# Tap loads over 119 partitions, layer-1 rows kept on chip, and the sums of the gates spread out, in a two-layer graph kernel on one core

## The chip, the cores and the metric

The kernel runs on one core of a Trainium2 chip, as one program. The metric is the device time of one execution in microseconds (us). The kernel before took 2211.03 us (median of 3 runs, 2210.8 to 2211.14).

## The reference, cut to what matters

There are 128 graphs (B) of 128 nodes (N) with 256 channels (D), all in float32. Layer 0 works on every node, layer 1 on the first 25 nodes of each graph.

```python
h = relu(layernorm(x))
# layer 0
c = relu(bn1(conv1x1(h)));  c = bn2(conv17(c))             # 17 taps along the nodes
x_conv = relu(c + h)
s = h @ w_se.T + b_se                                      # 3 numbers per node
A = exp(-|s_n - s_m|^2) * adj
x_nmp = A @ relu(h @ w_msg.T + b_msg)                      # "neighbours"
gi = concat(x_conv, x_nmp) @ w_ih.T + b_ih;  gh = h @ w_hh.T + b_hh
r, z = sigmoid(gi_r + gh_r), sigmoid(gi_z + gh_z)
x = x + (1 - z) * tanh(gi_n + r * gh_n) + z * h
# layer 1: for 5 groups g of nodes (25, 9, 7, 6 and 6 of the first 25 nodes)
h = relu(layernorm(x));  a = D^-1/2 (adj_g + I) D^-1/2
x[:, group] += w[g] * relu(a @ (relu(a @ (h @ W1[g]) + b1) @ W2[g]) + b2)
```

## The kernel before

**Units.** Layer 0 goes over 32 quads of 4 graphs (`q`). A quad's x is a tile of 128 partitions (4 graphs x 32 nodes) and 4 slices of 32 nodes; slice 0 holds the nodes that layer 1 needs. Layer 1 goes over 8 blocks of 16 graphs, that is 4 quads each (`blk`).

**Stage A** (L371-422, `stage_a`), once per quad, in two batches of 16: load x (`load_xa`, four DMAs on SyncE's queue), layernorm on VectorE (`moments`, `normalize`), transposes (`ph`, L390), the 1x1 convolution (`pc`, L401), and a real Fourier transform of length 80 along the nodes (`pf`, L412). h is written to DRAM (`hTd`).

**Tap weights** (L439-475, `tap_weights`), beside stage A of the first batch: the 17 taps of the convolution are brought to the 80 Fourier rows with matmuls whose contraction runs over the taps (`pw`, L455). Four of them work at the same time[...]. `load_taps` (L430) brings 64 input channels at a time into `wt`: in each of four bands of 32 partitions, 17 partitions (one per tap) take 16 channels. The 17th tap is a DMA of its own (L436). The products are copied to `ws` on VectorE and ScalarE and written to DRAM (`wfd`, L467, 4 KB runs).

**Stage B** (L478-533) multiplies in the Fourier domain, once per batch. **`early`** (L622) computes the neighbours (`pse`, `pm`, `pd`, `px`, L565-620) of each quad beside A and B and writes them to DRAM (`xmd`).

**Stage C** (L637-829), per quad: `stage_n` loads h and the neighbours back (`hT`, `xm`); `stage_c` does the inverse transform (`pi`), the transposes back (`pc`, L677), the gate products (`p`, L698), the product of h for the new state (`pg`, L762), and the sum with x (`po`, L814; L816-820). The gate matrices are multiplied by a Strassen-like scheme, so each operand of 2 x 2 blocks needs four differences on VectorE: `sums` (L547), called for the neighbours (`tm`, in `stage_n`, L644), for the convolution (`tc`, L735) and for h of the next quad (`th`, L767, after the product of h). The r and z gates are the seven products of `wrz`, the new state the seven of `wn` (L770-793), whose partial sums VectorE adds one after another (L777 to L793). The last steps of a quad's gates are six GpSimd instructions (L798-801).

**Layer 1** (L834-1067): `prepare(blk)` builds the normalised adjacency (`pa`, `pdg`, `pg` L962, `pr`), `rows_of_x` (L887) normalises the block's 16 x 32 rows of x: four `moments`, a power on GpSimd (L275), four scalings (L280) and one relu of 128x1024 on GpSimd (L901). The rows come from DRAM: `stage_c` writes slice 0 of each quad to `x1d` (L826), `load_x1` (L904) reads the block. Only the last block's rows are added in place (`direct`, L808). `block(blk)` then runs `py` (L986), five pairs of products (`ph` L1003, `pz` L1012), and per quad `pzt`, `pg2` (L1045), `pfu` (L1054) and the sum.

**What sets the order.** All engines run in order, and the order is written by `Order.run` (L176): lanes of generators yield (PE time of the step, time until the next step may be placed), and the lane with the least time done per weight goes next. In stage C the lanes are `groups` (weight 1), `beside` (0.5, the rest of `early`) and layer 1 (`second`, weight 0.36). So weights and yields decide only the order in which instructions stand in each engine's queue. A DMA lane is one of eight completion semaphores, shared by the DMAs of SyncE and ScalarE: each such DMA waits at its issue for the one eight before it.

Of the kernel before, what the change touches and what calls it, by code (L numbers as in the profile page):

```python
# [58 lines left out]
def _fourier():  # L59

    fwd = np.zeros((P, F, NB))
    inv = np.zeros((P, OB))
    tap = np.zeros((TAPS, F))
    i, t = np.arange(OB), np.arange(TAPS)
    for b in range(NB):  # L70
        for u in range(F):
            n = OB * b + u - PAD
            if 0 <= n < N:
                fwd[n, 0, b], fwd[n, 1, b] = 1, (-1) ** u
                for f in range(1, NF + 1):
                    th = 2 * np.pi * ((f * u) % F) / F
                    fwd[n, 2 * f, b], fwd[n, 2 * f + 1, b] = np.cos(th), -np.sin(th)
    inv[0], inv[1] = 1 / F, (-1.0) ** i / F
    for f in range(1, NF + 1):
        th = 2 * np.pi * ((f * i) % F) / F  # L80
        inv[2 * f], inv[2 * f + 1] = 2 / F * np.cos(th), -2 / F * np.sin(th)
    tap[:, 0], tap[:, NF + 1] = 1, (-1.0) ** t
    for f in range(1, NF + 1):
        th = 2 * np.pi * ((f * t) % F) / F
        tap[:, f] = -(np.cos(th) + np.sin(th)) / 2
        tap[:, NF + 1 + f] = (np.sin(th) - np.cos(th)) / 2
    tap4 = np.zeros((P, F))
    for r in range(4):
        tap4[32 * r:32 * r + TAPS] = tap
    return fwd.reshape(P, F * NB), inv, tap4  # L90
# [117 lines left out]
def kernel(ctx: ExitStack, tc: tile.TileContext, x, adj, consts, vecs, w_se, conv1_w,  # L208
# [17 lines left out]
    x1d = [dr.tile([SB, WIDE, D], FP, name=f"x1d{b}") for b in range(NBLK)]  # L226
# [144 lines left out]
    def stage_a(q):  # L371
        ab = LATE["ab"]
        for n in range(q, min(q + 2, (q // BQ + 1) * BQ)):
            if n not in XA:
                load_xa(n)
                if n == q:
                    yield 0.0, 6.0
# [19 lines left out]
        for h in range(2):  # L397
# [9 lines left out]
            yield 1.75, 2.0 * h  # L407
# [22 lines left out]
    def load_taps(n, *engines):  # L430

        wt = tw.tile([P, 16, D], FP, tag="wt", name=f"wt{n}")
        src = conv2_w.rearrange("(r n i) t o -> n t r i o", r=4, n=4)[n]
        for r in range(4):
            engines[r % len(engines)].dma_start(out=wt[32 * r:32 * r + 16], in_=src[:16, r])
        engines[0].dma_start(out=wt[16::32], in_=src[16])  # L436
        wts.append(wt)

    def tap_weights():  # L439

        yield 0.0, 0.0
        for n in range(4):
# [5 lines left out]
            for m in range(8):  # L448
# [4 lines left out]
                for r in range(4):  # L453
                    rows = slice(32 * r, 32 * r + TAPS)
                    nc.tensor.matmul(pws[r][:F], c("tap")[rows], wts[n][rows, 2 * m:2 * m + 2],  # L455
# [8 lines left out]
                if m % 2:  # L464
                    for r in range(4):
                        i0 = 64 * r + 16 * n + 2 * (m - 1)
                        nc.gpsimd.dma_start(out=wfd[:, i0:i0 + 4], in_=ws[:F, r])  # L467
# [68 lines left out]
    EN, IN, IN2, X1, E_DONE = {}, {}, {}, {}, set()  # L536
# [8 lines left out]
    TH, HT, TM = {}, {}, {}  # L545

    def sums(name, q, x, bufs=1):  # L547


        t = LATE["co"].tile([P, 4, D], FP, tag=name, name=f"{name}{q}", bufs=bufs)  # L550
        nc.vector.tensor_sub(t[:, 0], x[:, 0, D:], x[:, 0, :D])
        nc.vector.tensor_sub(t[:, 1], x[:, 1, D:], t[:, 0])  # L552
        nc.vector.tensor_sub(t[:, 2], x[:, 1, D:], x[:, 0, D:])
        nc.vector.tensor_sub(t[:, 3], t[:, 1], x[:, 1, :D])
        return t
# [81 lines left out]
    def stage_n(q):  # L637
# [5 lines left out]
        HT[q] = hT  # L643
        TM[q] = sums("tm", q, xm, bufs=2)  # L644
        IN[q] = hT, xm

    def stage_c(q):
        while not (q - 1 in G_DONE and q in IN):
            yield 0.0, 0.5
        (hT, xm), tm = IN.pop(q), TM.pop(q)  # L650
# [6 lines left out]
        th = TH.pop(q) if q in TH else sums("th", q, hT)  # L657
# [77 lines left out]
        tcs = sums("tc", q, xc)  # L735
# [3 lines left out]
        nc.vector.tensor_add(r2, r2, u2)  # L739
        yield 2.6, 0.0  # L740
        p5 = product(wrz, 4, xs)
        nc.vector.tensor_tensor(r2, r2, p5, ALU.add)  # L742
        sigmoid(r2, r2, 0)
        yield 2.6, 0.0
# [6 lines left out]
        sigmoid(z2, z2, 2)  # L751
        yield 2.6, 0.0
# [3 lines left out]
        sigmoid(z1, z1, 2)  # L756
        yield 2.6, 0.0

        for dc in range(2):
# [6 lines left out]
            if dc and q + 1 in HT:  # L766
                TH[q + 1] = sums("th", q + 1, HT.pop(q + 1))  # L767
# [40 lines left out]
        direct = X1.get(q // QS)  # L808
        for h in range(2):
# [6 lines left out]
            if h == 0 and direct is not None:  # L816
                nc.vector.tensor_add(direct[:, q % QS], xt[:, 0], po[:, 0])
                nc.vector.tensor_add(xt[:, 1], xt[:, 1], po[:, 1])
            else:
                nc.vector.tensor_add(xt[:, 2 * h:2 * h + 2], xt[:, 2 * h:2 * h + 2], po)  # L820
        yield 0.9, 1.5
        for j in range(GB):
            rows = xt[j * WIDE:(j + 1) * WIDE]
            g = q * GB + j
            if direct is None:
                nc.gpsimd.dma_start(out=x1d[g // SB][g % SB], in_=rows[:, 0])  # L826
            nc.gpsimd.dma_start(out=out[g, WIDE:].rearrange("(t n) c -> n t c", n=WIDE),
                                in_=rows[:, 1:4])
# [3 lines left out]
    S, B1_DONE, P_DONE, Y_DONE = {}, set(), set(), set()  # L832

    def setup_1():  # L834
# [39 lines left out]
        last = NBLK - 1  # L874
        X1[last] = S["pool2"].tile([P, QS, D], FP, tag="x1l", name=f"x1_{last}", bufs=1)
        P_DONE.add(-1)
        B1_DONE.add(-1)
        Y_DONE.add(-1)
# [8 lines left out]
    def rows_of_x(blk, wait=True):  # L887

        ready = all(q in C_DONE for q in range(blk * QS, (blk + 1) * QS))
        if blk in S or not (wait or ready and blk - 1 in Y_DONE):  # L890
            return
        while not (all(q in C_DONE for q in range(blk * QS, (blk + 1) * QS))
                   and blk - 1 in Y_DONE):
            yield 0.0, 0.5
        if blk not in X1:
            load_x1(blk)
            yield 0.0, 6.0
        pool2 = S["pool2"]
        x1h = S[blk] = pool2.tile([P, QS, D], FP, tag="x1h", name=f"x1h{blk}", bufs=1)
        normalize(x1h, X1[blk], *moments(X1[blk], "b"))  # L900
        nc.gpsimd.tensor_scalar(x1h, x1h, 0.0, None, op0=ALU.max)  # L901
        yield 0.0, 8.0 if wait else 0.0

    def load_x1(blk):  # L904
        X1[blk] = S["pool2"].tile([P, QS, D], FP, tag="x1", name=f"x1_{blk}")
        for j in range(GB):
            nc.sync.dma_start(out=X1[blk][j * WIDE:(j + 1) * WIDE],
                              in_=x1d[blk].rearrange("(q j) n c -> j n q c", j=GB)[j])

    def prepare(blk):  # L910
# [8 lines left out]
        if blk not in X1 and all(q in C_DONE for q in range(blk * QS, (blk + 1) * QS)):  # L919
            load_x1(blk)  # L920
# [33 lines left out]
        yield from rows_of_x(blk, wait=False)  # L954
# [17 lines left out]
        yield 0.9, 0.0  # L972
        yield from rows_of_x(blk)
        P_DONE.add(blk)

    def block(blk):
# [4 lines left out]
        x1, x1h = X1.pop(blk), S.pop(blk)  # L981

        for q in range(QS):
            py = ptmp.tile([P, 2, GB, NR], FP, tag="tmp", name=f"py{blk}_{q}")
            for cc in range(2):
                nc.tensor.matmul(py[:, cc], x1h[:, q, cc * P:(cc + 1) * P],  # L986
                                 r4[:, q].rearrange("p j r -> p (j r)"), start=True, stop=True)
            nc.vector.tensor_copy(yz[:, 0, q * GB:(q + 1) * GB, :NR], py[:, 0])  # L988
            nc.scalar.activation(yz[:, 1, q * GB:(q + 1) * GB, :NR], py[:, 1], AF.Copy)
            yield 0.75, 0.0 if q < QS - 1 else 2.4  # L990
        Y_DONE.add(blk)
# [24 lines left out]
        for g in range(NG + 1):  # L1016
# [6 lines left out]
            if g < NG:  # L1023
                load_w1(blk * NG + g + 2)

# [38 lines left out]
        for j in range(GB):  # L1064
            nc.gpsimd.dma_start(
                out=out[blk * SB:(blk + 1) * SB, :WIDE].rearrange("(q j) n c -> j n q c", j=GB)[j],
                in_=x1[j * WIDE:(j + 1) * WIDE])

# [4 lines left out]
    load_taps(0, nc.sync, nc.gpsimd, nc.scalar)  # L1073
    nc.scalar.dma_start(out=c1w, in_=conv1_w.rearrange("(k p) o -> p k o", p=P))
    load_xa(1)
    fold()
# [20 lines left out]
    order.run(groups, beside, Lane(second, ahead=2, weight=0.36))  # L1097
# [41 lines left out]
```

## Time and profile before

| stretch (us) | what runs | PE busy | granted clock | DMA share |
|---|---|---|---|---|
| 0 - 40 | start | 9.32 of 40 | 0.82 | 0.97 |
| 40 - 240 | stage A, first batch, tap weights | 186.14 of 200 | 0.94 | 0.76 |
| 240 - 400 | stage B, first batch | 159.57 of 160 | 1.00 | 0.79 |
| 400 - 580 | stage A, second batch | 165.65 of 180 | 0.96 | 0.52 |
| 580 - 745 | stage B, second batch | 165.00 of 165 | 1.00 | 0.77 |
| 745 - 1130 | stage C, layer 1 beginning | 370.79 of 385 | 0.98 to 1.00 | 0.33 to 0.42 |
| 1130 - 2136 | stage C with layer 1 | 981.75 of 1006 | 0.98 | 0.30 |
| 2136 - 2211 | last block of layer 1 | 41.57 of 75 | 0.79 | 0.11 |

The table is the answer for these stretches, with two of them added for 745 - 1130. PE busy is the time in which at least one matmul was under way; the granted clock says which share of TensorE's full clock the throttle gave; the DMA share is the mean busy share of the core's 16 DMA engines. Over the whole span PE is busy 94%, VectorE 54%, ScalarE 31%, GpSimd 36%.

### The profile page before, as it was taken

How to read it: one execution, taken by the hardware profiler on the slowest of the kernel's cores; microseconds unless marked ns; L12 is line 12 of the kernel's file. 1: busy time of each engine (PE TensorE's matmuls, PEld its weight loads, DVE VectorE, ACT ScalarE, POOL GpSimd, SP SyncE). 2: the span in 40 equal slices, each digit the busy share in tenths (PEclk: the TensorE clock that was granted, in tenths of full speed). 3: DMA queues.
4: the chain of work that ended last, by engine and by line, in shares of the span. 5: the costliest groups of instructions: out<-in, count | busy, mean ns of one | idle time of the engine just before them, and what ended most of it. 6: DMA issues, size and time to landing. Idle time of an engine off the chain costs nothing.

```text
span 2210.7 us, 30635 instructions
## 1 busy us (share of the span) xinstructions
PE 2079.8 (94%) x11124; PEld 1636.9 (74%) x11124; DVE 1198.4 (54%) x2659; ACT 690.1 (31%) x1511; POOL 788.4 (36%) x990
## 2 busy tenths in 40 slices
PE   4999999899999999999999999999999999999967
PEld 2667888788888777777767778677777777776855
DVE  3765444676444547654554564564564565465541
ACT  2654222344322333223322322322322322322322
POOL 2431466231465234333332342252242333333140
PEclk8999999999999999999999999999999999999988
DMA  9986777744777734323232333232332322332211
GB/s 163 267 244 195 237 262 259 215 144 134 238 261 253 229 92 121 84 71 89 76 103 79 91 90 88 65 94 84 86 91 69 94 75 80 101 85 71 77 34 39
DMA packets 194359, 288.97 MB, mean 131 GB/s; under 512 B 22877, under 2 KB 145762, under 8 KB 194210
## 3 DMA queue, kind: packets, MB, share of 16 engines
q1 hardware_dynamic: 159794, 188.48, 30.0%
q0 software_dynamic: 33584, 97.81, 14.0%
q8 instruction: 88, 1.44, 0.3%
q10 hardware_dynamic: 832, 0.74, 0.2%
q14 instruction: 61, 0.50, 0.1%
HBM read 191.01 MB, written 95.94 MB: 130 GB/s over the span
## 4 chain that ended last, share of the span: by engine, by line
PE 83%; DVE 7%; DMA 4%; issue 2%; POOL 2%; ACT 1%; SPq 1%; DVEq 0%; ACTq 0%; POOLq 0%
PE p L698 33%; PE pa L502 6%; PE pg L762 5%; PE ph L1003 5%; PE pz L1012 5%; PE pm L591 4%; PE pc L401 4%; PE pb L502 3%; PE pi L663 3%; PE px L616 2%; PE pf L412 2%; DMA xa<-in_x 2%; PE pg L1045 1%; PE pc L677 1%; DVE st L272 1%
## 5 line engine op out<-in xcount | busy, mean ns | idle before, releaser
L798 POOL TENSOR_TENSOR d<-hTc,r 128x512 f32<-128x512 f32 x64 | 84.3, 1317 | 508.4 <-ACT r L795 495.7
L502 PE MATMUL pa<-wf,X 128*128 128x256 f32 x640 | 154.2, 385 | 0.0
L698 PE MATMUL p<-tc,wrz 128*128 128x256 f32 x512 | 133.0, 382 | 1.5 <-DVE tc L552 1.0
L698 PE MATMUL p<-th,wrz 128*128 128x256 f32 x512 | 134.2, 385 | 0.0
L698 PE MATMUL p<-tm,wrz 128*128 128x256 f32 x512 | 133.2, 383 | 0.0
L502 PEld LDWEIGHTS pa<-wf,X 128*128 128x128 f32 x640 | 119.3, 192 | 17.5 <-issue 2.8
L275 POOL TENSOR_TENSOR rs<-rs,cst 128x4 f32<-128x4 f32 x40 | 42.0, 1049 | 250.7 <-DVE rs L274 243.6
L525 DVE SCALAR_TENSOR_TENSOR y<-pa,kk 128x512 f32<-128x512 f32 x78 | 53.8, 690 | 142.7 <-ACT kk L524 142.5
L401 PE MATMUL pc<-c1w,hTa 128*128 128x256 f32 x512 | 127.6, 399 | 0.3 <-ACT hTa L392 0.3
L591 PE MATMUL pm<-wmsg,hT 128*128 128x256 f32 x512 | 121.2, 381 | 0.0
L401 PEld LDWEIGHTS pc<-c1w,hTa 128*128 128x128 f32 x512 | 98.3, 199 | 29.2 <-issue 6.4
L711 ACT ACTIVATE r<-r,brz 128x256 f32<-128x256 f32 x128 | 58.0, 500 | 186.5 <-DVE r L742 157.3
L762 PE MATMUL pg<-hTc,whn 128*128 128x512 f32 x256 | 116.0, 593 | 0.0
L826 POOL DMA_DIRECT2D x1d<-xt x112 | 59.3, 530 | 150.5 <-DVE xt L820 147.2
L698 PEld LDWEIGHTS p<-tc,wrz 128*128 128x128 f32 x512 | 97.5, 192 | 17.9 <-DVE tc L552 4.7
L1003 PE MATMUL ph<-yz,w 128*128 128x96 f32 (+3 forms) x640 | 108.3, 322 | 0.5 <-DVE yz L988 0.5
L698 PEld LDWEIGHTS p<-tm,wrz 128*128 128x128 f32 x512 | 98.5, 192 | 13.7
L1012 PE MATMUL pz<-hh,w 128*128 128x96 f32 (+3 forms) x640 | 107.4, 321 | 0.0
L698 PEld LDWEIGHTS p<-th,wrz 128*128 128x128 f32 x512 | 94.8, 190 | 16.9 <-issue 4.9
L591 PEld LDWEIGHTS pm<-wmsg,hT 128*128 128x128 f32 x512 | 95.9, 190 | 15.3 <-issue 2.1
L698 PE MATMUL p<-tm,wn 128*128 128x256 f32 x256 | 80.6, 397 | 24.2 <-DVE v L777 24.2
L1003 PEld LDWEIGHTS ph<-yz,w 128*128 128x128 f32 x640 | 87.1, 190 | 21.8 <-issue 15.8
(198 smaller groups left out, 4587.4 us busy)
## 6 DMA issues: line engine op xcount, KB each, us to landing
wf<-wfd SPq DMA_DIRECT2D x160, 256.0 KB, 4.0
wfd<-ws POOLq DMA_DIRECT2D x64, 320.0 KB, 6.2
yd<-y POOLq DMA_DIRECT2D x80, 256.0 KB, 3.8
yt<-yd SPq DMA_DIRECT2D x64, 320.0 KB, 4.1
w<-in_W SPq DMA_DIRECT2D x40, 512.0 KB, 4.0
xa<-in_x SPq DMA_DIRECT2D x128, 128.0 KB, 4.7
hTd<-hTa POOLq DMA_DIRECT2D x32, 512.0 KB, 4.8
hT<-hTd SPq DMA_DIRECT2D x32, 512.0 KB, 6.5
```

Of the source, the lines that this page charges most:

```text
L401: nc.tensor.matmul(pc[:, i], hT[:, k, (2 * h + i) * N:(2 * h + i + 1) * N], c1w[:, k], start=(k == 0), stop=(k == 1))
L502: nc.tensor.matmul(ps, xk(k), WF[f][:, k, s], start=(k == 0), stop=(k == 1))
L525: nc.vector.scalar_tensor_tensor(y, pa, 2.0, kk[:, None].to_broadcast([P, 2, D]), op0=ALU.mult, op1=ALU.subtract)
L591: nc.tensor.matmul(pm[:, i], hT[:, k, j * N:(j + 1) * N], wmsg[:, k], start=(k == 0), stop=(k == 1))
L663: nc.tensor.matmul(pi[b * 64:(b + 1) * 64], inv[:F], yt[:, b::2], start=True, stop=True)
L698: nc.tensor.matmul(ps[:, m], w[:, i, k, m * P:(m + 1) * P], factor(i, x, t), start=first and j == 0, stop=last and j == len(n) - 1)
L711: nc.scalar.activation(dst[:, m], src[:, m], AF.Sigmoid, bias=brz[:, b + m:b + m + 1])
L762: nc.tensor.matmul(pg, whn[:, k, dc * P:(dc + 1) * P], hT[:, k], start=(k == 0), stop=(k == 1))
L798: nc.gpsimd.tensor_sub(d, hT[:, dc], r[:, dc])
L826: nc.gpsimd.dma_start(out=x1d[g // SB][g % SB], in_=rows[:, 0])
L1003: nc.tensor.matmul(ph, w1[:, k, m * P:(m + 1) * P], yz[:, k, :, o:o + n], start=(k == 0), stop=(k == 1))
L1012: nc.tensor.matmul(pz, w2[:, g, m, cc * P:(cc + 1) * P], hs[g][:, m], start=(m == 0), stop=(m == 3))
```

## The change

It is a change in five parts.

1. **Taps in 119 partitions.** `wt` holds, for eight channels c, a pair s of channels: partition 17 j + t of slot (c, s) is tap t of channel 8 c + j + s. One DMA per s, of 119 partitions x 8 x 256, on SyncE's and GpSimd's queues; no 17th tap apart. A matmul of band r reads partitions 32 r to 34 r + 16, and the tap matrix has zeros in the rows that are not its own. Channels are loaded twice (except the first and last of eight), and `wfd` is written in runs of 2 KB rather than 4 KB.
2. **Order of the start.** x of quads 0 and 1 and the 1x1 weights are asked for ahead of the taps, x of quad 2 behind the first taps; `tap_weights` is placed 18 us later; two yields of `stage_a` are longer.
3. **Rows on chip.** No `x1d`: `stage_c` always adds slice 0 into a tile `X1[blk]` (three buffers). `rows(q)`, a lane of its own, normalises one quad's 32 x 4 rows after that quad, with the relu on ScalarE. `py` of a block's quad waits for its own quad alone.
4. **Sums spread.** The eight sums of h and neighbours of quad q + 1 are placed in ones and twos after the gate products of quad q (`some_sums`); `th` and `tm` have two buffers.
5. **Layer 1's weight** 0.36 becomes 0.2.

```diff
-        tap4[32 * r:32 * r + TAPS] = tap
+        tap4[34 * r:34 * r + TAPS] = tap
...
-                    yield 0.0, 6.0
+                    yield 0.0, 14.0 if q > BQ else 6.0
...
-        wt = tw.tile([P, 16, D], FP, tag="wt", name=f"wt{n}")
-        src = conv2_w.rearrange("(r n i) t o -> n t r i o", r=4, n=4)[n]
-        for r in range(4):
-            engines[r % len(engines)].dma_start(out=wt[32 * r:32 * r + 16], in_=src[:16, r])
-        engines[0].dma_start(out=wt[16::32], in_=src[16])
+        wt = tw.tile([P, 8, 2, D], FP, tag="wt", name=f"wt{n}")
+        src = conv2_w[64 * n:64 * (n + 1)].rearrange("(c j) t o -> (j t) c o", j=8)
+        for s in range(2):
+            engines[s].dma_start(out=wt[:7 * TAPS, :, s], in_=src[s * TAPS:(s + 7) * TAPS])
...
-        yield 0.0, 0.0
+        yield 0.0, 18.0
...
-                    rows = slice(32 * r, 32 * r + TAPS)
-                    nc.tensor.matmul(pws[r][:F], c("tap")[rows], wts[n][rows, 2 * m:2 * m + 2],
+                    rows = slice(32 * r, 34 * r + TAPS)
+                    nc.tensor.matmul(pws[r][:F], c("tap")[rows], wts[n][rows, m],
...
-                        nc.gpsimd.dma_start(out=wfd[:, i0:i0 + 4], in_=ws[:F, r])
+                        nc.gpsimd.dma_start(
+                            out=wfd.rearrange("f (c r s) o -> f r c s o", r=4, s=2)
+                            [:, r, 8 * n + m - 1:8 * n + m + 1],
+                            in_=ws[:F, r].rearrange("f (c s) o -> f c s o", s=2))
...
+    def some_sums(q, n):
+        if q in IN:
+            if q not in SUMS:
+                hT, xm = IN[q]
+                (th, a), (tm, b) = sums("th", q, hT), sums("tm", q, xm)
+                SUMS[q] = th, tm, a + b
+            while SUMS[q][2] and n != 0:
+                SUMS[q][2].pop(0)()
+                n = n and n - 1
...
-        TM[q] = sums("tm", q, xm, bufs=2)
...
+        some_sums(q + 1, 1)
         yield 2.6, 0.0
...
-            if dc and q + 1 in HT:
-                TH[q + 1] = sums("th", q + 1, HT.pop(q + 1))
+            some_sums(q + 1, 1)
...
+        blk = q // QS
+        while blk > 2 and blk - 3 not in F_DONE:
+            yield 0.0, 0.5
+        if blk not in X1:
+            X1[blk] = fr.tile([P, QS, D], FP, tag="x1", name=f"x1_{blk}", bufs=3)
...
-            if direct is None:
-                nc.gpsimd.dma_start(out=x1d[g // SB][g % SB], in_=rows[:, 0])
...
-        normalize(x1h, X1[blk], *moments(X1[blk], "b"))
-        nc.gpsimd.tensor_scalar(x1h, x1h, 0.0, None, op0=ALU.max)
...
+    def rows(q):
+        while not (q in C_DONE and -1 in P_DONE and (q < 8 or q - 8 in PY_DONE)):
             yield 0.0, 0.5
+        x1 = X1[q // QS][:, q % QS]
...
+        nc.vector.bn_stats(st, x1)
+        nc.vector.bn_aggr(mv, st)
+        nc.vector.tensor_scalar(rs, mv[:, 1:2], EPS, None, op0=ALU.add)
+        nc.gpsimd.tensor_tensor(rs, rs, c("mhalf")[:, :1], ALU.pow)
+        yield 0.0, 2.5
+        x1h = S["x1h", q] = S["pool"].tile([P, D], FP, tag="x1h", name=f"x1h{q}", bufs=8)
+        nc.vector.tensor_scalar(x1h, x1, mv[:, 0:1], rs, op0=ALU.subtract, op1=ALU.mult)
+        nc.scalar.activation(x1h, x1h, AF.Relu)
...
     load_xa(0)
-    load_taps(0, nc.sync, nc.gpsimd, nc.scalar)
     nc.scalar.dma_start(out=c1w, in_=conv1_w.rearrange("(k p) o -> p k o", p=P))
     load_xa(1)
+    load_taps(0, nc.sync, nc.gpsimd)
+    load_xa(2)
     fold()
...
-    order.run(groups, beside, Lane(second, ahead=2, weight=0.36))
+    order.run(groups, beside, Lane([rows(q) for q in range(NQ)], ahead=2),
+              Lane(second, ahead=2, weight=0.2))
```

## The prediction

> **What bounds the kernel now.** I read the page's first two parts, then the stretches of 20 us, then what PE waited for, then two timelines. On the page:
>
> ```profile
> PE 2079.8 (94%) x11124; PEld 1636.9 (74%) x11124; DVE 1198.4 (54%) x2659; ACT 690.1 (31%) x1511; POOL 788.4 (36%) x990
> PE   4999999899999999999999999999999999999967
> PEclk8999999999999999999999999999999999999988
> DMA  9986777744777734323232333232332322332211
> ```
>
> PE bounds it: 94% busy, idle 2210.7 - 2079.8 = 131 us. Both builds hold the same matmuls (2739 rows of PE in the written order), so the change can only take idle time, or time at a low clock, out of PE. Where that lies, by stretches of 20 us (columns: length, PE, PEld, DVE, ACT, POOL busy, clock, DMA share, GB/s):
>
> ```profile
> 0.00:20.00 20.00, 4.45 (x24) 3.59 (x24) 6.30 (x29) 2.48 (x3) 4.13 (x9) 1.00 1.03 143
> 20.00:40.00 20.00, 4.88 (x20) 2.00 (x16) 6.30 (x21) 1.66 (x4) 2.62 (x3) 0.64 0.91 127
> 80.00:100.00 20.00, 17.99 (x96) 12.05 (x95) 12.96 (x31) 11.29 (x24) 7.01 (x13) 0.91 0.94 307
> 1100.00:1120.00 20.00, 15.15 (x52) 11.15 (x52) 13.04 (x32) 3.28 (x7) 6.20 (x7) 0.86 0.43 126
> ```
>
> At the start DMA is full but moves only 127 to 143 GB/s, against 307 at the same share later. In stage C about one 20 us stretch in nine loses 5 us and some clock. The waits of PE name the causes:
>
> ```profile
> PE p L698 <- DVE v L777: 24.2, 5, 4.8
> PE pw L455 <- DVE ws L462: 15.1, 1, 15.1
> PE p L698 <- DVE v L783: 9.2, 2, 4.6
> PE py L986 <- POOL x1h L901: 8.6, 1, 8.6
> PE ph L390 <- issue: 8.3, 1, 8.3
> PE po L814 <- POOL z L801: 8.1, 2, 4.7
> ```
>
> One of the seven stops in stage C, as timeline:
>
> ```profile
> 1108.08 0.42 DVE L272 BATCH_NORM_STATS2 st<-x 128x6 f32<-128x256 f32 x1
> ...
> 1111.66 1.38 DVE L280 TENSOR_SCALAR x1h<-x,mv,rs 128x256 f32<-128x256 f32 x4 [1.16 <-POOL rs L275]
> 1112.95 0.42 DVE L551 TENSOR_TENSOR tm<-xm 128x256 f32<-128x256 f32 x1
> 1113.41 1.14 DVE L552 TENSOR_TENSOR tm<-xm,tm 128x256 f32<-128x256 f32 x1
> ...
> 1115.14 0.41 DVE L777 TENSOR_TENSOR v<-v,p 128x256 f32<-128x256 f32 x1
> ...
> 1115.61 1.22 PE L698 MATMUL p<-tm,wn 128*128 128x256 f32 x2 [4.84 <-DVE v L777]
> ```
>
> A block's whole layernorm and the four `tm` sums, 7 us in all, stand in VectorE's queue ahead of L777; PE has filled its three gate banks by 1110.76 and stands.
>
> [...] after that stop the `wn` pairs follow each other at 0.85 us rather than 0.43. [...] No trace here shows a transfer of 119 partitions. [...] the `th` sums at 0.91-0.95 us mean, beside the GpSimd gates, against 0.42 of the `tc` sums agree.
>
> **Stage C (parts 3 and 4).** Removed: seven stops, 24.2 + 9.2 = 33.4 us, and the half clock after them. The stretches from 920 to 2020 us lose, as 20 us x (1 - clock), 1.8, 2.8, 0.6, 1.8, 1.8, 3.4, 1.8, 1.2, 0.6, 1.2, 2.2 and 1.8 = 21.0 us; about 1 lies inside the stops, so 20. Together 53. Added per quad: moments 0.42 + 0.18 + 0.17 and a scaling 0.41 on VectorE, one power on GpSimd (1.05), one relu of 128x256 on ScalarE (about 0.4, as L775). The new wait is the scaling for that power. Ahead of it on GpSimd stand the quad's four output issues, 4 x 0.56 = 2.2 us, so it is ready some 3.3 us after the last sum with x, while the order places the scaling 2.5 us later: VectorE may stand about 1 us. Queued behind are the r and z sums, each with 2.6 us of PE product before its bank is wanted, so PE should not see it. In the new order the work of VectorE between the product of h and L777 is at most 2.8 us where it was up to 5.8; a block's `prepare` now falls into `wn` more often (3 to 5 us in all, spread over 6 to 10 us of PE). I charge 5 us, bounds 0 and 20. Also gone at no gain to the path: 112 issues to `x1d` (59.3 us of GpSimd), eight relus of 2.8 us, and SyncE's waits on the read back. Net -48.
>
> **The start (parts 1 and 2).** PE runs 9.3 us of work before 38.25, then is dense. The first stop ends when VectorE, having waited for x of quad 2 until 35.18, frees the banks of `pw`. After: x of 0 and 1 and the 1x1 weights go ahead of SyncE's taps, but GpSimd's taps start at 1.3 us as before. By the packets' own times in the trace, one of 1 KB took 46 ns where nothing limits it (107 to 124 in the first 40 us): x of quad 0 is 32 of them per engine, 1.5 us, plus the others' share, so it lands near 8 to 10 us, not 12. `pc` then starts 5.4 + 2.7 us later, near 17 (20.1 before). A tap half is 952 packets; over seven engines 136 x 46 ns = 6.3 us; x of quad 2 queues behind it and lands near 19. Its moments stand in front of `h` on VectorE, so PE stands from about 20 to 23, then is dense with the same work done: `ph`, two `pc`, no `pw`, against `ph`, one `pc`, six of eight `pw`. That is 38.2 - 23 = 15 us; bounds 5 and 20.
>
> **Stage A's rest.** Later tap halves put 6.3 us on seven engines beside `wfd`, whose queue takes about two thirds of the DMA there: landing up to 20 us against 7 to 12. The x loads of quads 8 and 12 are queued behind them; about 22 us of PE work lie between the issue and the transposes that need that x, of which 5 us are VectorE's. I charge 4 us, bounds 0 and 15. Runs of 2 KB in `wfd` move the same bytes; 4 KB packets took 159 ns and 1 KB 46, the same per byte, so 0. More taps (1904 KB a set against 1088) cost nothing of PE beyond this: `pw` keeps its columns.
>
> **Second batch.** `ph <- issue` is 8.3 us: at 403.9 to 411.0 VectorE does the moments of three quads before the first scaling at 413.5. With 14 us in two yields, quad 16's moments and scaling come first, and 3.4 us more of `pm` stand ahead. It gains about 6 of the 8.3 us and 1.5 of the clock: -7.5, bounds -2 and -10.
>
> **The tail (part 5).** At 2136.2, when the last gates end, before has one block left, which waits for the quad's GpSimd gates (4.7 + 3.4), moments, power, relu (8.6) and runs at half clock to 2159. In the new order blocks 6 and 7 are left. After the last gates PE would do: `pfu` and `py` 2.7, a copy 0.8, block 6 36.0 (as 2160.6 to 2196.6), `po`, `pa`, `pg`, `pr` 2.4, then `py` 2.5, 0.6 and block 7 36.0, and 14.1 to the end: 95.1 us against 74.5. But block 6's 37.3 us of PE work (1.9 + 25.4 + 7.5 of back transforms, 2.5 of the rest) left the time before. Net 95.1 - 74.5 - 37.3 = -17; bounds -5 and -20. The last quad's rows are hidden behind block 6.
>
> Sum: 2211 - 48 - 15 + 4 - 7.5 - 17 = 2127.5, so **2128**.
>
> **Rivals.** (a) The seven-engine loads stall stage A at start, quads 8 and 12: start gains 5, rest costs 15: 2128 + 10 + 11 = 2149. For: DMA share 0.9 to 1.0 up to 140 us. [...] (b) VectorE's stop is only moved: `prepare` or the power hits `wn` in half the quads, so 27 of 53 us stay: 2128 + 22 = 2150. For: the 1672 ns power and 4 sums with `dm`. Against: 2.8 us at most ahead of L777. (c) All bounds good: 2211 - 53 - 20 - 10 - 20 = 2108. (d) Slower: GpSimd or SyncE puts 119 partitions on one engine: 952 x 46 ns = 44 us a half, x behind it; four sets stretch stage A by 25 us each, 2128 + 100 + 15 = 2243.
>
> **Chances.** Forecast 0.55, (a) 0.17, (b) 0.13, (c) 0.1, (d) 0.05. Faster 0.93, same 0.02, slower 0.05. The range holds all but (d) and the ends of the others where two come together: 2092 to 2172.
>
> **What would show it.** Right: no `p <- v` wait over 2 us in stage C, its clock at 1.00; first dense PE near 23 us and over 200 GB/s there; `ph` of quad 16 with under 3 us; two blocks after the last gates and no `py <- x1h` wait. Wrong: `ph` or `st` waiting for `xa` by tens of us between 60 and 150, or a tap load landing after 30 us.

## The result, and the profile after

The changed kernel took 2244.94 us (median of 4 runs, 2237.26 to 2247.7), the kernel before 2211.09 beside it: a ratio of 1.0134, 95% interval 1.009 to 1.0177. It is slower by some 30 us; the forecast was 2128, with 2092 to 2172 as range.

The page of the changed kernel, busy time first, then PE, its clock and DMA in 40 slices:

```profile
PE 2104.6 (94%) x11124; PEld 1651.7 (74%) x11124; DVE 1315.7 (59%) x2711; ACT 704.1 (31%) x1545; POOL 736.8 (33%) x891
...
PE   4889999999999999999999999999999999999998
...
PEclk8979999999999999999999999999999999999999
DMA  7878778644678534222223223213222232222121
```

PE has the same 11124 instructions and 25 us more busy time: the same matmuls ran longer, and some 20 of the 25 us are work at the half clock (worked out as for the table below). VectorE has 52 instructions and 117 us more. The first three stretches shown of before, the next one, and one of stage C (length, then PE, PEld, DVE, ACT, POOL busy, clock, DMA share, GB/s):

```profile
0.00:20.00 20.00, 7.78 (x30) 6.54 (x31) 7.42 (x31) 2.48 (x3) 5.17 (x8) 1.00 0.85 162
20.00:40.00 20.00, 3.77 (x16) 2.97 (x15) 7.84 (x27) 0.91 (x2) 2.62 (x3) 0.62 0.82 162
80.00:100.00 20.00, 16.55 (x91) 10.65 (x90) 12.38 (x33) 9.59 (x21) 10.25 (x13) 0.92 0.93 270
100.00:120.00 20.00, 13.98 (x56) 8.67 (x55) 7.12 (x19) 5.73 (x12) 5.71 (x9) 0.76 0.62 197
1680.00:1700.00 20.00, 17.55 (x79) 13.14 (x76) 14.67 (x22) 7.33 (x14) 8.14 (x6) 0.91 0.30 86
```

The start is not much denser (11.6 of 40 us busy against 9.3), and the first batch has a hole after 100 us that was not there. Around 1700 us stage C loses 2.4 us in every second such stretch, and in most of these some clock; 40 us are about one quad with its share of layer 1. What PE waited for (line numbers shift from kernel to kernel: the gate products are L698 in the kernel before and L706 here):

```profile
PE p L706 <- ACT xc L691: 47.1, 22, 4.0
PE pw L453 <- ACT ws L458: 17.5, 5, 6.7
PE ph L389 <- issue: 16.2, 1, 16.2
PE prow L301 <- DVE wide L300: 12.2, 1, 12.2
```

The seven stops for `v` are gone, as forecast. In their place stand 22 stops for `xc`, the convolution's result, 47.1 us in all. One of them in the timeline:

```profile
1683.17 0.42 DVE L553 TENSOR_TENSOR th<-hTc 128x256 f32<-128x256 f32 x1
...
1683.30 1.41 POOL L811 TENSOR_TENSOR d<-hTc,r 128x512 f32<-128x512 f32 x1 [14.25 <-ACT r L808]
1683.62 1.38 DVE L553 TENSOR_TENSOR th<-hTc,th 128x256 f32<-128x256 f32 x1
...
1684.79 1.33 POOL L812 TENSOR_TENSOR d<-d,z 128x512 f32<-128x512 f32 x1
1684.92 1.49 DVE L553 TENSOR_TENSOR th<-hTc 128x256 f32<-128x256 f32 x1
...
1686.42 1.04 PE L685 MATMUL pc<-cst,xi 128*128 128x128 f32 x8
...
1691.96 0.41 DVE L553 TENSOR_TENSOR tm<-tm,xm 128x256 f32<-128x256 f32 x1
1692.30 1.65 DVE L688 SCALAR_TENSOR_TENSOR xc<-pc,s_bn,hTc 128x256 f32<-128x256 f32 x4
...
1693.36 4.54 PE L706 MATMUL p<-xc,wrz 128*128 128x256 f32 x12 [2.45 <-ACT xc L691]
```

All eight sums `th` and `tm` of a quad stand on VectorE ahead of its `xc` (L688), from 1683.17 to 1692.37, 9.2 us. The transposes `pc` that `xc` needs are done by 1687.5; `xc` begins at 1692.30, PE stands 2.45 us, and the twelve products after it take 4.54 us (2.75 at full clock, below). Why 9.2 us: while the six GpSimd operations of the last quad's gates run (1.32 to 1.44 us each), one sum gets through per GpSimd operation. Six of the eight sums take 1.37 to 1.49 us, the first and the last 0.42 and 0.41. By what means the one engine holds up the other the trace does not show.

That the sums stand there is in the written order of VectorE, and I had not looked for it. From quad 5 on, seven or eight of the sums stand there in every quad (H a sum of h, M of the neighbours, x one of the operations of `xc`, c a sum of the convolution, numbers the gate product whose result is added there, g the product of h, w the new state; layer 1's instructions are left out):

```
changed:  HHHHMMMM xxxx cccc [5]   [4]    [6]   [3]    [g]  [g]  [w]
meant:             xxxx cccc [5] H [4] HH [6] H [3] MM [g] M [g] M [w]
```

The diff calls `some_sums(q + 1, ...)` after each product, but the call does nothing unless quad q + 1 is in `IN`. `stage_n(q + 1)` begins only when `stage_c(q - 1)` has ended, whose last steps (L818 on) are placed 11 us and more after its last gate product, and it sets `IN` 7 us or more after that. In the planner's own time quad 19 begins at 1462.5, `stage_c(18)` ends at 1479.1, the last call for the sums of quad 20 comes at 1486.1 and `IN` at 1490.6: too late by 4.5. While `early` still runs beside stage C some sums are placed in time; later next to none, and the call at the head of `stage_c` (L658) puts them all there.

**Where the time went.** For a common measure I add up, by stage, PE's idle time and half of its busy time at the half clock, which is what that work would have saved at the full one; both come from the records of one profiled run of each kernel. The clock records of the kernel before and of the changed one hold two values alone, 1 and 0.5; in the kernel before, matmuls on 128x256 start a median of 216 ns apart under the first and 427 ns under the second. Stage bounds are the first and last product of stage B, the first inverse transform and the last gate product.

| lost PE time (us) | 0-40 | rest of first A | first B | second A | second B | stage C | tail | sum |
|---|---|---|---|---|---|---|---|---|
| before | 31.6 | 25.2 | 1.7 | 18.6 | 3.1 | 53.5 | 36.1 | 169.8 |
| changed | 30.0 | 40.3 | 0.0 | 14.7 | 5.4 | 95.5 | 11.1 | 197.0 |
| experiment 1 | 29.5 | 39.6 | 0.0 | 14.7 | 5.5 | 15.6 | 9.4 | 114.3 |
| experiment 8 | 23.7 | 18.6 | 0.0 | 14.6 | 5.5 | 19.0 | 13.1 | 94.5 |

Stage C lost 42 us more where the forecast had 48 less, the first batch 15 more, the tail 25 less. The sum gives +27 of the 32 us between the two spans (2210.7 and 2242.6). The last two rows are of kernels told of below.

### The profile page after: what moved, and what is told of

Same layout as the page of the kernel before. It is cut to its first block, busy times and chain, and to the rows that moved or that the text cites. A ratio compares the mean times of both kernels' runs of the same rounds, so it can differ in the third digit from the quotient of the medians.

```text
span 2242.6 us, 30416 instructions
## 1 busy us (share of the span) xinstructions
PE 2104.6 (94%) x11124; PEld 1651.7 (74%) x11124; DVE 1315.7 (59%) x2711; ACT 704.1 (31%) x1545; POOL 736.8 (33%) x891
## 3 DMA queue, kind: packets, MB, share of 16 engines
q8 instruction: 88, 1.44, 0.3%
## 4 chain that ended last, share of the span: by engine, by line
PE 76%; DVE 14%; DMA 4%; issue 2%; ACT 2%; POOL 1%; SPq 0%; POOLq 0%; DVEq 0%; ACTq 0%
PE p L706 29%; PE pa L502 6%; DVE th L553 5%; PE pg L776 5%; PE ph L1007 5%; PE pm L601 4%; PE pz L1016 4%; DVE tm L553 4%; PE pc L400 4%; PE pb L502 3%; DMA xa<-in_x 3%; PE px L626 2%; PE pf L411 2%; PE pg L1050 1%; PE po L831 1%
## 5 line engine op out<-in xcount | busy, mean ns | idle before, releaser
L811 POOL TENSOR_TENSOR d<-hTc,r 128x512 f32<-128x512 f32 x64 | 88.5, 1384 | 401.7 <-ACT r L808 401.6
L840 POOL DMA_DIRECT2D out<-xt x128 | 72.1, 568 | 321.2 <-DVE xt L837 310.2
L706 PE MATMUL p<-xc,wrz 128*128 128x256 f32 x384 | 115.2, 459 | 47.2 <-ACT xc L691 47.1
L706 PEld LDWEIGHTS p<-xc,wrz 128*128 128x128 f32 x384 | 86.3, 231 | 74.2 <-ACT xc L691 58.1
L706 PE MATMUL p<-tc,wrz 128*128 128x256 f32 x512 | 131.6, 379 | 4.4 <-DVE tc L553 4.4
L706 PE MATMUL p<-th,wrz 128*128 128x256 f32 x512 | 133.7, 384 | 0.0
L706 PE MATMUL p<-tm,wrz 128*128 128x256 f32 x512 | 131.8, 380 | 0.0
L691 ACT ACTIVATE xc<-xc,t_bn 128x256 f32<-128x256 f32 x128 | 54.5, 496 | 202.1 <-DVE xc L688 202.1
L706 PEld LDWEIGHTS p<-tc,wrz 128*128 128x128 f32 x512 | 97.1, 190 | 18.3 <-DVE tc L553 5.2
L1009 ACT ACTIVATE hh<-ph,vec 128x96 f32<-128x96 f32 (+3 forms) x160 | 64.2, 403 | 145.3 <-PE ph L1007 136.4
L601 PEld LDWEIGHTS pm<-wmsg,hT 128*128 128x128 f32 x512 | 95.9, 190 | 17.6 <-issue 2.5
L706 PEld LDWEIGHTS p<-tm,wrz 128*128 128x128 f32 x512 | 97.8, 191 | 13.5
```

The source lines that it names most:

```text
L601: nc.tensor.matmul(pm[:, i], hT[:, k, j * N:(j + 1) * N], wmsg[:, k], start=(k == 0), stop=(k == 1))
L706: nc.tensor.matmul(ps[:, m], w[:, i, k, m * P:(m + 1) * P], factor(i, x, t), start=first and j == 0, stop=last and j == len(n) - 1)
L811: nc.gpsimd.tensor_sub(d, hT[:, dc], r[:, dc])
L840: nc.gpsimd.dma_start(out=out[q * GB + j, WIDE:].rearrange("(t n) c -> n t c", n=WIDE), in_=xt[j * WIDE:(j + 1) * WIDE, 1:4])
L1009: nc.scalar.activation(hh[:, m], ph, AF.Relu, bias=v("b1", g * 4 + m))
```

## The experiments

Theory 1: the eight sums ahead of `xc` cost stage C its time. Theory 2: the rows of layer 1 (a power on GpSimd, a relu on ScalarE, a scaling per quad) do. Theory 3: stage C's loss is a by-product, and the taps and the start set the result. A fourth, the lower weight of layer 1, is tested in experiment 2.

Times are medians; each ratio is to the kernel before on the same chip, which took 2213.8 to 2215.7 there.

**1. Sums really spread.** The loads of quad q + 1 are placed as soon as the gates of q - 1 are placed.

```diff
     def stage_n(q):
+        while q > 1 and q - 2 not in G_DONE:
+            yield 0.0, 0.5
...
-    groups = Lane([stage(q) for q in range(NQ) for stage in (stage_n, stage_c)], ahead=2)
+    groups = Lane([stage(q) for q in range(NQ) for stage in (stage_n, stage_c)], ahead=3)
```

> The changed kernel, with the loads of a quad's h and neighbours (stage_n) placed as soon as the gates of the quad two before are done, so that its eight sums really stand in ones and twos after the gate products of the quad before it; in the changed kernel all eight stood ahead of xc from the seventh quad on. Theory 1 (the eight sums in front of xc cost stage C its time): the wait of the gate products for xc falls from 47.1 us to under 5, no wait for v of over 2 us comes back, the idle and half-clock loss between the first inverse transform and the last gates falls from 95 to about 40 us: 2243 - 55 = 2188, range 2178 to 2202. Theory 2 (the rows of layer 1, with their power on GpSimd and relu on ScalarE, are what slows VectorE and PE): the loss moves to another place, 2225 or more. Theory 3 (only the start and the taps matter): within 5 us of 2243.

Measured: 2158.79 us, ratio 0.9749 (0.9728 to 0.977), 86 us less than the changed kernel. The written order is now the line "meant" above. The `th` sums in the changed kernel between 1200 and 2000 us, by form (min/median/max ns, first and last start):

```profile
L553 DVE TENSOR_TENSOR th<-hTc x38: 418/1424/1498, 1219.2 to 1979.2; 128x256 f32<-128x256 f32 x38
L553 DVE TENSOR_TENSOR th<-hTc,th x19: 424/1382/1497, 1219.7 to 1977.9; 128x256 f32<-128x256 f32 x19
L553 DVE TENSOR_TENSOR th<-th,hTc x19: 1480/1489/1494, 1222.4 to 1980.6; 128x256 f32<-128x256 f32 x19
```

The same in experiment 1:

```profile
L553 DVE TENSOR_TENSOR th<-hTc x40: 416/419/421, 1208.7 to 1968.4; 128x256 f32<-128x256 f32 x40
L553 DVE TENSOR_TENSOR th<-hTc,th x20: 416/418/420, 1211.4 to 1968.1; 128x256 f32<-128x256 f32 x20
L553 DVE TENSOR_TENSOR th<-th,hTc x20: 416/418/421, 1214.7 to 1971.4; 128x256 f32<-128x256 f32 x20
```

Not one sum is slowed any more. What PE still waits for in its stage C (765 to 2064 us), whole list but for waits under half a microsecond:

```profile
PE py L992 <- ACT x1h L914: 4.3, 4, 3.3
PE p L708 <- DVE tc L553: 4.1, 2, 3.6
```

The loss of stage C falls from 95.5 to 15.6 us. Theory 1 holds; I had put what would remain at 40, so the gain was larger than expected, and the time lies below the range. Theory 2 (the rows' power and relu) is out: they are all still there. So is theory 3, for the taps and the start are as in the changed kernel.

**2. Layer 1's weight back at 0.36** (`weight=0.2` to `weight=0.36`, nothing else).

> The changed kernel with layer 1's weight back at 0.36. Theory 1 (sums in front of xc): three of four quads still have seven or eight sums ahead of xc, so about three quarters of the wait for xc stay, 35 us; with the tail about 10 us longer and stage C about 15 us shorter, 2238, range 2228 to 2248. Rival (the low weight itself made stage C slow): the wait for xc falls under 10 us and the time to about 2200.

Measured: 2238.06 us, ratio 1.0102 (1.008 to 1.0123). Of its waits:

```profile
PE p L706 <- ACT xc L691: 29.2, 13, 2.5
...
PE py L990 <- ACT x1h L912: 15.9, 23, 7.6
```

As theory 1 has it, most of the wait for `xc` stays (29.2 of 47.1 us), so the low weight is not what brings it. It does add to it: with the higher weight stage C loses 67.6 us instead of 95.5, and the tail 27.4 instead of 11.1.

**3. Sums as before** (neighbours in `stage_n`, h after the product of h if loaded by then, else ahead of `xc`); parts 1, 2, 3 and 5 stay.

```diff
+        TM[q], todo = sums("tm", q, xm)
+        for operation in todo:
+            operation()
...
+        if q not in TH:
+            th_sums(q, hT)
...
-            some_sums(q + 1, 1)
+            if dc and q + 1 in IN:
+                th_sums(q + 1, IN[q + 1][0])
```

> The changed kernel with the sums as before: the four of the neighbours in stage_n, the four of h after the product of h or, where that comes too early, ahead of xc. Parts 1, 2, 3 and 5 stay. Four sums instead of eight then stand ahead of xc in most quads, and the four of the neighbours between the product of h and the new state in most. Theory 1: the wait for xc falls from 47.1 to about 10 us, but stops for v of 4 to 5 us come back in some quads (10 to 30 us in all): 2243 - 20 = 2223, range 2205 to 2235. Theory 2 (rows): the loss of stage C stays near 95 us, 2240 or more.

Measured: 2157.53 us, ratio 0.9736 (0.9718 to 0.9754). I had expected 2223: neither the stops for `v` nor those for `xc` come. In its stage C (763 to 2067 us) PE waits for little:

```profile
PE p L705 <- DVE tc L558: 4.1, 2, 3.7
PE py L986 <- ACT x1h L908: 3.4, 4, 2.8
```

In most quads four sums still stand ahead of `xc`, and most of them are slow (the `th` sums have a median of 1378 to 1486 ns), yet PE does not wait; eight are too many. And the four of the neighbours stand ahead of `v` in most quads without a stop, now that no layernorm of a whole block stands there with them. So part 4 was not needed to remove the seven stops.

**4. Parts 1 and 2 alone on the kernel before** (the edit goes on with the start, the yields and `wfd`).

```diff
-        for r in range(4):
-            engines[r % len(engines)].dma_start(out=wt[32 * r:32 * r + 16], in_=src[:16, r])
-        engines[0].dma_start(out=wt[16::32], in_=src[16])
+        for s in range(2):
+            engines[s].dma_start(out=wt[:7 * TAPS, :, s], in_=src[s * TAPS:(s + 7) * TAPS])
...
```

> The kernel before with parts 1 and 2 alone (taps in 119 partitions, order of the start, the two yields). As the trace of the changed kernel has it (start 2 us less lost, rest of the first batch 16 us more, second batch 2 to 4 us less): 2211 + 11 = 2222, range 2214 to 2228. As the forecast had it (start -15, rest of the first batch +4, second batch -7.5): 2192.

Measured: 2226.95 us, ratio 1.0055 (1.0036 to 1.0074): a loss of about 12 us, not a gain. Its profiled run was the slowest of the four, 4 us over the median. In that run the first 40 us lose 1 us less than before, the rest of the first batch 9.5 more, the second batch 3.9 less, and stage C 15 more. The last was not expected, for from the fifth quad on the sums and gates of stage C stand on VectorE as before; its stops are as before too:

```profile
PE p L699 <- DVE v L778: 24.2, 5, 4.8
...
PE p L699 <- DVE v L784: 9.5, 2, 5.0
```

These are the 33.4 us of before, but 57 us of busy PE fall under the half clock where it was 36, and more of `early` is left for stage C (its last `pse` comes 63.4 us after the first inverse transform, before 36.6). That this is all of the 15 us was not tried, and some of it may be chance of that run.

**5. Sums spread, parts 1 and 2 undone** (experiment 1 with the taps and the start as before).

> The kernel of the first experiment (sums really spread) with parts 1 and 2 undone: taps in four bands of 17 partitions and the start as before. If parts 1 and 2 cost what they cost on the kernel before (12 us, the ratio of that run), 2159 - 12 = 2147, range 2139 to 2153, which beats every kernel so far. If they help once stage C is clean, over 2160.

Measured: 2157.41 us, ratio 0.9742 (0.9727 to 0.9757), the same as experiment 1, and between the two times expected. With stage C clean, parts 1 and 2 neither gain nor lose: without them the first 40 us and the rest of the first batch lose 13 us less, the second batch 4 and stage C 10 more (25.2 against 15.6).

**6. Parts 3 and 5 alone on the kernel before.**

> Parts 3 and 5 alone on the kernel before: rows on chip and layer 1's weight at 0.2; sums, taps and start as before. The loss of stage C as in the third experiment (20 us) and of the tail (9), the start as before: 2147, range 2139 to 2153. Part 4, spread as meant, is then worth the difference to the run with the sums spread and the old taps: 0 to 5 us if only stops of the sums count.

Measured: 2156.3 us, ratio 0.9734 (0.9717 to 0.975), just outside the range, with a loss of stage C of 24.5 us rather than 20. The spread of experiment 5 is worth nothing on top.

**7. Part 3 alone** (experiment 6 with the weight at 0.36).

> Part 3 alone on the kernel before: rows on chip, weight 0.36. If part 3 (no whole layernorm of a block ahead of v) removed the seven stops: no wait for v over 2 us, 8 us for py behind x1h and po behind z as in the run with weight 0.36, loss in stage C some 30 and in the tail 27: 2211 - 33 = 2178, range 2168 to 2190. If it was part 5 (layer 1 in smaller shares) that removed them: the waits for v stay over 20 us and the time is 2195 or more.

Measured: 2183.29 us, ratio 0.9855 (0.9839 to 0.9871). Its five longest waits in stage C (760 to 2117 us):

```profile
PE p L704 <- ACT xc L689: 6.4, 1, 6.4
PE py L985 <- ACT x1h L907: 5.7, 22, 0.3
PE pa L934 <- POOL b L923: 3.2, 1, 3.2
PE pi L669 <- DMA yt<-yd: 1.0, 2, 0.6
PE p L704 <- DVE v L791: 1.0, 2, 0.5
```

So part 3 removed the seven stops, and is worth 32 us; part 5 on top of it (experiment 6) is worth 27: the loss of the tail falls by 15 (25.0 to 9.7) and that of stage C by 5 (29.3 to 24.5); the rest does not show in this measure.

**8. The tap halves in 112 and 7 partitions.** Experiment 1 with each half as two transfers.

```diff
-            engines[s].dma_start(out=wt[:7 * TAPS, :, s], in_=src[s * TAPS:(s + 7) * TAPS])
+            for a, b in ((0, 112), (112, 119)):
+                engines[s].dma_start(out=wt[a:b, :, s], in_=src[s * TAPS + a:s * TAPS + b])
```

> The kernel of the first experiment with each tap half as two transfers, of partitions 0 to 111 and of 112 to 118 [...]; same bytes, same place in the queues. In the changed kernel seven of the 16 completion marks of every x transfer near a tap half came 4 to 7 us after the other nine, and SyncE's tap half landed 23 us after its issue. If the seven engines are the cause: the SyncE half lands under 14 us after its issue, x of quad 2 near 27 us instead of 33, and the first batch loses 8 to 15 us less: 2147, range 2141 to 2153. If it is the bytes and the later tap products (18 us) that cost, the time stays within 4 us of 2159.

Measured: 2133.7 us, ratio 0.9629 (0.9614 to 0.9643): 25 us less than experiment 1, and more than expected. The trace has, for each transfer, the times of its completion marks. Each part of x below has sixteen, as many as the core has DMA engines, so I take a mark for the report of one engine. In the changed kernel and in this one:

```
changed  GpSimd's first tap half, asked for at 1.40:   nine at 9.75 to 10.75, seven at 17.71 to 18.64
changed  x of quad 1, third part, asked for at 4.48:   nine at 11.30 to 11.84, seven at 17.77 to 18.68
changed  SyncE's first tap half, asked for at 9.01:    one at 9.51, seven at 30.65 to 31.97
changed  x of quad 2, first part, asked for at 9.39:   nine at 22.44 to 27.61, seven at 31.02 to 32.22
exp. 8   SyncE's 112 partitions, asked for at 13.44:   sixteen at 18.74 to 19.82
```

SyncE's half of 119 partitions has eight marks: seven 21.6 to 23.0 us after the issue, and one 0.5 us after it, too soon for even a sixteenth of its 952 packets at 46 ns (2.7 us). The 112 partitions of experiment 8 have sixteen, 5.3 to 6.4 us after it. From this I take it that seven engines carried the half and sixteen the 112 partitions. And x of quad 2, asked for right behind that half, has its seven late reports when that half has them. The split of x of quad 1 is not that half's doing as far as the trace tells, for x was asked for earlier; its late reports come with those of GpSimd's half, which splits in nine and seven as well. What this does to x of quad 2, on VectorE in the changed kernel:

```profile
33.48 0.43 DVE L271 BATCH_NORM_STATS2 st<-xa 128x6 f32<-128x256 f32 x1 [11.53 <-DMA xa<-in_x]
```

and in experiment 8:

```profile
26.29 0.43 DVE L271 BATCH_NORM_STATS2 st<-xa 128x6 f32<-128x256 f32 x1 [5.76 <-DMA xa<-in_x]
```

The loss falls from 29.5 to 23.7 in the first 40 us and from 39.6 to 18.6 in the rest of the first batch. There PE stood for `pw <- ws`, 17.5 us in the changed kernel and 8.9 in experiment 8. In the changed kernel the trace leads one step further: ScalarE, which empties `pw` into `ws`, waited for `ws` to be written out to `wfd`:

```profile
ACT ws L458 <- DMA wfd<-ws: 27.5, 5, 9.6
```

That is the changed kernel, 40 to 240 us, with 9.6 us as the longest; in experiment 8 it is 20.2 in seven waits, 6.5 the longest, and the slowest write of `wfd` lands after 10.8 us instead of 17.6. But VectorE, which empties the other part of `pw`, waits longer for these writes, 22.2 us instead of 11.9, so in sum the two engines wait no less. That the loss goes with the halves in one piece is shown; that it comes by way of these writes is not.

**9. The eight sums in one bunch**, elsewhere (experiment 1 with `some_sums(q + 1, None)` after product 6 and no other call).

> The kernel of the first experiment with all eight sums of the next quad in one bunch, after the product 6 of wrz, instead of in ones and twos. If it is the place that counts (in front of xc, and beside the GpSimd operations of the gates, where a sum took 1.4 us instead of 0.42), the bunch is 8 x 0.42 = 3.4 us at a point where PE has gate banks left: no stop, 2159, range 2153 to 2166. If a bunch of eight stops PE wherever it stands, each of 31 quads loses 1 us or more: 2190 or more.

Measured: 2170.83 us, ratio 0.9799 (0.9769 to 0.9828), about 11 us over experiment 1 and 74 under the changed kernel. It lies between the two expectations, near the first: every sum takes 0.42 us, no stop for a sum comes, and the wait of `py` for the rows grows from 4.3 to 11.1 us. Why was not tried. The place counts far more than the bunching.

**10. One more stop taken out of the best kernel.** Experiment 8 with the moments of quad 2 placed behind the two `h` of quad 0.

```diff
+        if q == 2:
+            yield 0.0, 9.0
         if q not in MOM:
```

> The kernel of the eighth experiment (sums spread, tap halves in 112 and 7 partitions) with the moments of quad 2 placed 9 us later, behind the two sums h of quad 0 on VectorE. In the eighth run PE stood 6.9 us (22.9 to 29.7) because these moments, waiting for x of quad 2 until 26.3, stood ahead of h. If that is the reason, the gap shrinks to 2 us or less and the time goes to 2129, range 2124 to 2133; if x of quad 2 is needed by PE at once anyway, it stays at 2134.

Measured: 2137.25 us, ratio 0.9644 (0.9621 to 0.9668): no gain. The stop is gone (6.9 to 1.1 us), and the first 40 us lose 16.3 instead of 23.7; but the rest of the batch loses 26.8 instead of 18.6, mostly at the half clock. What PE gained ahead it gave back; which wait took it was not followed further.

**11. Sums behind `xc`.** The changed kernel with its eight sums right after the four operations of `xc`, still at the same time.

```diff
-        some_sums(q, None)                      # head of stage_c
...
                 turn_back()
+                some_sums(q, None)
```

> The changed kernel with the eight sums placed right behind xc (the four operations that make it from the transposes) instead of ahead of it; all else as changed, so the loads of h and neighbours still come late. If only the delay of xc costs, the stop goes: 2170, range 2160 to 2185. If VectorE is the limit in this stretch (ten us of sums, slowed by the GpSimd operations of the gates, have to be done between the gates of one quad and product 5 of the next, wherever they stand), the stop moves from xc to the sums tc of product 5: the wait for xc falls under 5 us, one of 30 to 80 us for tc comes, and the time stays at 2215 to 2245.

Measured: 2170.78 us, ratio 0.9797 (0.978 to 0.9815): 74 of the 86 us come back from this alone. The same quad as in the timeline above, in this kernel:

```profile
1687.41 1.66 DVE L687 SCALAR_TENSOR_TENSOR xc<-pc,s_bn,hTc 128x256 f32<-128x256 f32 x4 [3.81 <-PE pc L684]
...
1688.98 0.41 DVE L553 TENSOR_TENSOR th<-hTc 128x256 f32<-128x256 f32 x1
1689.04 1.48 POOL L814 TENSOR_TENSOR d<-d,z 128x512 f32<-128x512 f32 x1
...
1689.43 1.37 DVE L553 TENSOR_TENSOR th<-hTc,th 128x256 f32<-128x256 f32 x1
...
1691.10 2.75 PE L705 MATMUL p<-xc,wrz 128*128 128x256 f32 x12
```

`xc` begins 4.9 us earlier, and four of the six GpSimd operations are over when the sums begin, so only two of the eight are slow (1.37 and 1.48 us); the rest take 0.41 to 0.43. PE does not stop, and its twelve products take 2.75 us. VectorE was never the limit in this stretch; its order was.

**12. Parts 1 and 2 on the kernel before, the halves split** (experiment 4 with the split of experiment 8).

> The kernel before with parts 1 and 2, the tap halves as two transfers of 112 and 7 partitions. On the kernel of the first experiment that made 25 us (2159 to 2134); parts 1 and 2 alone cost the kernel before 12 us. If the seven engines were what made parts 1 and 2 a loss: 2211 + 12 - 25 = 2198, range 2190 to 2206, so that these parts, given 16 engines, gain about what the forecast gave them (-18.5). If the loss of parts 1 and 2 on the kernel before has another cause (work moved into stage C), 2210 to 2222.

Measured: 2194.17 us, ratio 0.9899 (0.988 to 0.9917): 22 us gained where experiment 4 lost 12. So it was the halves of 119 partitions in one piece that made these parts a loss. The first 40 us and the rest of the first batch lose 21.0 and 21.4 us, against 30.6 and 34.7 in experiment 4. Stage C still loses some 10 us more than in the kernel before (63.9, in the slowest of the four runs), so some of experiment 4's loss has another cause.

In sum, against the kernel before (ratio less 1, times 2211):

| parts | us |
|---|---|
| 1, 2 | +12 |
| 1, 2 with 112 + 7 partitions | -22 |
| 3 | -32 |
| 3, 5 | -59 |
| 1, 2, 3, 5 | -58 |
| all five, as changed | +30 |
| all five, the sums really spread | -55 |
| all five, the sums really spread, 112 + 7 partitions | -82 |

The last, experiment 8, is the fastest of all; experiment 10 can't be told from it.

## Why the prediction was wrong

**Stage C (-48).** This is the step that failed. It read from the new order that at most 2.8 us of VectorE work stand between the product of h and L777, and that was right: no stop for `v` is left. But it took from the diff, not from the order, that the eight sums lie in ones and twos behind the gate products; it put the moved sums at nothing and looked for new waits only in the scaling behind the power. The sums stood ahead of `xc`, a place I did not look at, and cost 86 us (changed kernel against experiment 1; against experiment 3, which also differs in the sums alone, 87). The prediction itself quoted 0.91 to 0.95 us for the `th` sums beside the GpSimd gates, against 0.42 for those of `tc`; eight of these in a row ahead of anything that PE waits for should have been an alarm. Where the sums really are spread, stage C's loss is 15.6 us against 53.5, so -38 for the -48 forecast.

The reasons given inside the step were right in part: that part 3 removes the stops (experiment 7), and that the rows' power, relu and scaling hardly reach PE (some 4 us in `py <- x1h` in experiment 1).

**The start (-15; measured -1.6).** That seven engines carry a tap half was an assumption that no trace of the kernel before could show; the changed kernel's trace, with its seven late marks (experiment 8), bears it out. It was priced too low: 136 packets an engine (952 over seven) at 46 ns are 6.3 us, and the tap half took 23.0, or 169 ns for each of the 136, with x under way beside it. The packets of 1 KB on SyncE's queue took a mean of 95 ns from 9.5 to 32 us, not 46. The rate of an unloaded engine was put in where everything was loaded. So x of quad 2 landed at 33.4, not 19, and PE was dense at 37, not 23; with the halves split it was dense at 29.7 (experiment 8). One of the prediction's own signs of being wrong, a tap load landing after 30 us, was there (31.97).

**Rest of the first batch (+4, bounds 0 and 15; measured +15.1).** At the bound, and the place was wrong: PE stood not for x of quads 8 and 12 but for `ws` ahead of `pw`, and `ws` for the writes of `wfd`. It goes with the halves of 119 partitions in one piece: experiment 8 takes 21 us of this loss away. By which waits is open, as said there.

**Second batch (-7.5; measured -3.9).** The stop of 8.3 us is gone; smaller ones follow it, and 2.3 us more are lost before stage C begins.

**The tail (-17; measured -25).** Right, and better than priced: 91.4 us from the last gates to the end where 95.1 were worked out, with two blocks left and no wait for the rows. In the prediction's own sum that is 91.4 - 74.5 - 37.3 = -20.4, just past its bound of -20.

**Rivals.** (a) named the right culprit for the start and the first batch, with 21 us lost to the forecast; they lost 13.4 + 11.1 = 24.5. (b) said that VectorE's stop would be moved rather than removed, and that is what happened, but in nearly every quad and ahead of `xc`, where (b) had half the quads and `wn`; so it ended at 2150. Only (d) ended above 2211, and that its 2243 is close to what was measured is luck, for its cause did not come. What was missing is a rival in which the moved work costs more at its new place than at the old one.

With the sums really spread and the tap halves split the ratio is 0.9629, and 0.9629 x 2211 = 2129, the time that was forecast. That too is luck in part, for the terms don't match: the first 40 us gained 8 us (forecast 15), the rest of the first batch gained 7 (a loss of 4), stage C gained 34 (48) and the tail 23 (17).

## What to carry to other kernels

Where a generator or a scheduler writes the order, look up in that order where every moved instruction ends up, and ask of each what stands behind it; a call of the form "if it is ready" may do nothing, and its work then lands all at once where it can't be put off any more. Here VectorE sums of two SBUF operands went at the pace of GpSimd's operations beside them (1.37 to 1.49 us instead of 0.42), so in such a stretch put first what PE waits for. Here a transfer of 119 partitions on SyncE's queue had seven late completion marks, one of 112 sixteen, and the split in 112 and 7 took 25 us off the kernel's time. So when a change gives a transfer another number of partitions, count its marks in the trace, and try a split if they are few.

## What the runs showed of the hardware that I had not expected

- Beside a chain of GpSimd operations on 128x512, a VectorE sum of two SBUF operands of 128x256 took 1.37 to 1.49 us instead of 0.42, one per GpSimd operation; GpSimd itself hardly slowed (mean 1384 ns for `d` against 1317 before). The operations of `xc`, which read one operand from PSUM, stayed at 0.41 (1.66 us for four, beside the same GpSimd chain).
- On SyncE's queue the issue right behind each tap half of 119 partitions (952 packets, 136 an engine if seven share them) lasted 10.49 and 9.15 us, and delayed the next parts of x by that. Right behind the transfers of 112 partitions (896 packets, 56 an engine over sixteen) in experiment 8 they lasted 0.50 and 0.74 us. Why was not tried.
- Seven stops for `v` of nearly the same length went with different lengths of busy PE at the half clock in stage C: 33.4 us of stops with 36 us in the kernel before, 33.7 with 57 in experiment 4, 34.5 with 45 in experiment 12 (one run each; the last two had some 6 us of other stops besides). What decides it was not tried.
